# When the experts of a layer pair start, how evenly their work is spread, and how PSUM banks are handed out

## The chip, the cores and the metric

The kernel runs on one core of a Trainium2 chip. A core has five engines with instruction queues of their own: TensorE (PE, matmuls and transposes into PSUM), VectorE (DVE), ScalarE (ACT), GpSimd (POOL) and SyncE (SP, which here only issues DMAs). [...]The metric is the device time of one execution in microseconds (us), lower is better.

## The reference

The input is 16 sequences of 512 tokens with 256 features. Two layers follow each other, each with a residual and a layernorm. All arithmetic is float32.

The first layer is a bidirectional state-space block:

```
xr = x @ in_proj_w.T ; xf, res = split(xr)                # 512 channels each
xf = silu(conv4(xf))   ; y   = ssm(xf, forward weights)
xb = silu(conv4b(xf))  ; y_b = ssm(xb, backward weights, reversed in time)
x = layernorm(x + ((y + y_b) * silu(res)) @ out_proj_w.T)
# ssm: delta = softplus(..); for each of 16 states n:
#   dA = delta * A[n] ; dB_u = delta * u * B[n] ; xs = scaled cumulative sum of dB_u under the decays
#   y += xs * C[n] ; then y += u * D
```

The second layer is a soft mixture of 16 experts with 64 slots each (1,024 slots), with weights of three matrices per expert (256x512, 256x512, 512x256):

```
logits = layernorm(x) @ se.T                              # 512 tokens x 1024 slots
slots  = softmax over tokens (dispatch).T @ layernorm(x)
eout   = (gelu(slots @ Wg + bg) * (slots @ Wu + bu)) @ Wd + bd
x = layernorm(x + softmax over slots (combine) @ eout)
```

## The kernel before

**The scan.** For each sequence `b` of 16 there are four calls of `scan_part` (direction `r`, half of the channels `p`). A part has 8 pairs of states and two chunks of 128 channels, so 16 scan steps; a sequence has 64 and the kernel 1,024. A step does the following. POOL multiplies `du` with the broadcast row `bs` into `db` (L427). ScalarE computes two decays `exp` (L444) and two factors `tanh` (L446). VectorE runs two `tensor_tensor_scan` into the PSUM tiles `h` (L450 forward, L452 backward), each followed by a product with the factor into one half of `hg` (L455). POOL multiplies `hg` with the broadcast row `cs` (L456). PE adds the transposed result into the accumulator `acc` (L371) two steps later. Buffers: `h` 3 PSUM tiles, `th`, `db`, `bs` and `cs` 3 each, `hg` 4. For the states 5 and 13 the term comes from PE instead (`by_diagonal`, L405, from `dg` and `duT`) and lies in a PSUM bank from its matmul to the scan that reads it.

**Side work.** Everything else is written as Python generators, run piece by piece between the scan steps by `beside_scan` (L541). There are three queues, objects of class `Side`: `prep` (projections, convolution taps and steps of the parts to come), `front` (`finish`: output projection, layernorm and `dispatch` of the sequence before) and `back` (`experts` and `combine`). A generator yields the number of PSUM banks that its next piece needs; GAP added to it means not in the step in which something of this queue was taken up; HOLD means that the piece's banks are still to be read, which is done at the next step; WAIT means nothing before the next step. In each step every held or waiting queue is taken up (`take_up`), then `prep` may do a piece, then `front` and `back` each do one if they have at least 1.0 credit. Credit grows each step by the pieces left divided by the scan steps left (`paced_piece`, L524).

**Banks.** Side work and `by_diagonal` share 3 PSUM banks in one rotating pool. `count` numbers all banks handed out, and a piece may run if the number handed out since the oldest hold, with its own need, is at most 3 (L510, L511).

**Layer pairs.** Sequences 2g and 2g+1 share one pass `experts(g)` over all expert weights, in 8 steps of two experts: `pg` (L825, L830), Gelu, `pu` (L779), product, `peo` (L806), store. `combine` of each of the two follows: 4 blocks of tokens with `cl` (L884), Exp, `ctp` (L905) and `cpo` (L962). Slots go through DRAM: `dispatch` writes `s_dram` in four quarters (L738), and `experts` reads them in `load_slots` (`st`, one buffer, L766). `experts(g)` is added at the start of sequence 2g+3, when the dispatch of sequence 2g+1 is complete, to be spread over 128 steps; that of sequences 12 and 13 has only the 64 steps of sequence 15.

**Tail.** Behind the last scan, five more banks and more SBUF come free. `side_by_side` (L1033) then runs `front` and `back` in turns, in three rounds: `finish(15)` beside what `back` has left and the combine weights of sequence 14; the last experts beside the weights of 15; the two combines.

**Order of instructions.** A planner of the framework orders each engine's instructions by program order and its own model of what is ready; an instruction in `late(...)` keeps its place in program order. DMAs of SP are queued in the same way.

## Time and profile before

| What | Value |
|---|---|
| time, median of 3 runs | 5415.38 us (5413.15 to 5421.7) |
| time of the profiled execution | 5411.23 us |
| its span, first to last instruction | 5409.4 us |
| POOL, VectorE, PE, ScalarE busy | 87%, 84%, 80%, 76% |
| mean granted PE clock | 0.889 |
| DMA | 907.7 MB, mean 168 GB/s |

Rows of groups give line, engine, operation, tiles and shapes, the count, busy us, the mean ns of one, and the idle time of the engine ahead of them with what ended it. Rows of stretches give, for a stretch in us from the start of the span, its length, the busy time of each engine with the number of instructions, the granted PE clock, and the share and rate of the DMA engines. Rows of waits give who waited for whom, the us in total, the number of waits and the longest. Rows in order of time give start, duration, engine, line and operation. Queue names with a q (ACTq) are an engine's issue of a DMA.

### The profile page before, as it was taken

How to read it: one execution, taken by the hardware profiler on the slowest of the kernel's cores; microseconds unless marked ns; L12 is line 12 of the kernel's file. 1: busy time of each engine (PE TensorE's matmuls, PEld its weight loads, DVE VectorE, ACT ScalarE, POOL GpSimd, SP SyncE). 2: the span in 40 equal slices, each digit the busy share in tenths (PEclk: the TensorE clock that was granted, in tenths of full speed). 3: DMA queues.
4: the chain of work that ended last, by engine and by line, in shares of the span. 5: the costliest groups of instructions: out<-in, count | busy, mean ns of one | idle time of the engine just before them, and what ended most of it. 6: DMA issues, size and time to landing. Idle time of an engine off the chain costs nothing. (4 is left out here: it accounts for less than half of the span.)

```text
span 5409.4 us, 73721 instructions
## 1 busy us (share of the span) xinstructions
PE 4331.1 (80%) x24144; PEld 3390.0 (63%) x24145; DVE 4559.7 (84%) x6276; ACT 4087.2 (76%) x6515; POOL 4732.1 (87%) x2537
## 2 busy tenths in 40 slices
PE   5656666898888978788888977889787897888889
PEld 3445555676666666677656765667656776667657
DVE  7888988889898899888998888988899889988722
ACT  6677777787888778887877887788788887877641
POOL 6999999999999899998999989998999989988600
PEclk7778778898899988899888989899889998989999
DMA  4334333575446644566446754467444764457436
GB/s 137 131 117 137 125 129 131 189 230 159 156 142 212 225 149 148 158 223 213 131 144 194 232 170 153 132 212 232 149 149 146 225 224 134 145 179 234 126 103 188
DMA packets 595236, 907.73 MB, mean 168 GB/s; under 512 B 78082, under 2 KB 384898, under 8 KB 594852
## 3 DMA queue, kind: packets, MB, share of 16 engines
q1 hardware_dynamic: 521156, 859.87, 49.5%
q10 hardware_dynamic: 73696, 43.14, 2.8%
q8 instruction: 192, 3.15, 0.2%
q14 instruction: 192, 1.57, 0.1%
HBM read 840.86 MB, written 62.01 MB: 167 GB/s over the span
## 5 line engine op out<-in xcount | busy, mean ns | idle before, releaser
L456 POOL TENSOR_TENSOR hg<-hg,cs 128x1024 f32<-128x1024 f32 x1024 | 2420.8, 2368 | 128.1 <-DVE hg L455 110.0
L427 POOL TENSOR_TENSOR db<-du,bs 128x1024 f32<-128x1024 f32 (+1 forms) x1024 | 2144.4, 2098 | 232.3 <-DVE h L450 84.7
L371 PE MATMUL acc<-ident,hg 128*128 128x128 f32 x8192 | 1179.3, 295 | 203.3 <-POOL hg L456 181.6
L455 DVE SCALAR_TENSOR_TENSOR hg<-th,h 128x512 f32<-128x512 f32 x1792 | 1185.8, 678 | 177.2 <-PE acc L371 90.4
L371 PEld LDWEIGHTS acc<-ident,hg 128*128 128x128 f32 x8192 | 1044.9, 154 | 390.8 <-POOL hg L456 240.9
L452 DVE TENSOR_TENSOR_SCAN h<-h,db 128x512 f32<-128x512 f32 x896 | 1072.8, 1218 | 112.2 <-ACT h L444 107.5
L450 DVE TENSOR_TENSOR_SCAN h<-h,db 128x512 f32<-128x512 f32 x896 | 1071.1, 1217 | 48.8 <-ACT h L444 45.7
L446 ACT ACTIVATE th<-rr,Ah_f 128x512 f32<-128x512 f32 x1024 | 725.0, 714 | 186.3 <-DVE hg L455 183.1
L446 ACT ACTIVATE th<-rr,Ah_b 128x512 f32<-128x512 f32 x1024 | 721.5, 712 | 155.2 <-DVE hg L455 147.7
L444 ACT ACTIVATE h<-dt,A_f 128x512 f32<-128x512 f32 x896 | 608.2, 680 | 117.5 <-DVE hg L455 112.6
L444 ACT ACTIVATE h<-dt,A_b 128x512 f32<-128x512 f32 x896 | 608.6, 681 | 108.8 <-DVE hg L455 105.1
L687 PE MATMUL pl<-x2T,seT 128*128 128x512 f32 x512 | 299.1, 715 | 78.7 <-DVE hg L455 37.4
L405 PE MATMUL hd<-dg,duT 128*128 128x128 f32 x2048 | 305.6, 298 | 32.7 <-ACT yt L627 13.5
L830 PEld LDWEIGHTS pg<-st,Wg 128*128 128x128 f32 x2048 | 244.8, 196 | 106.2 <-issue 85.0
L405 PEld LDWEIGHTS hd<-dg,duT 128*128 128x128 f32 x2048 | 283.1, 214 | 38.4 <-ACT yt L627 15.7
L806 PE MATMUL peo<-Wd,ht 128*128 128x256 f32 x1024 | 257.0, 407 | 55.6 <-DVE rr L337 38.6
L779 PE MATMUL pu<-st,Wu 128*128 128x128 f32 x2048 | 254.5, 283 | 50.1 <-DMA Wu<-in_Wu_dram 32.7
L962 PE MATMUL cpo<-ceo,ct 128*128 128x256 f32 x1024 | 254.8, 407 | 46.9 <-DVE rr L337 39.9
L779 PEld LDWEIGHTS pu<-st,Wu 128*128 128x128 f32 x2048 | 244.9, 198 | 61.5 <-DVE h L452 24.2
L830 PE MATMUL pg<-st,Wg 128*128 128x128 f32 x2048 | 269.9, 286 | 4.1 <-DMA Wg<-in_Wg_dram 3.1
L884 PE MATMUL cl<-seT,cx 128*128 128x512 f32 x512 | 244.7, 617 | 32.5 <-DVE res L272 12.3
L806 PEld LDWEIGHTS peo<-Wd,ht 128*128 128x128 f32 x1024 | 205.3, 206 | 97.7 <-DVE rr L337 41.2
(154 smaller groups left out, 6654.8 us busy)
## 6 DMA issues: line engine op xcount, KB each, us to landing
cs<-bc SPq DMA_DIRECT2D x512, 512.0 KB, 3.9
bs<-bc SPq DMA_DIRECT2D x384, 512.0 KB, 5.1
Wg<-in_Wg_dram SPq DMA_DIRECT2D x128, 512.0 KB, 6.0
Wu<-in_Wu_dram SPq DMA_DIRECT2D x128, 512.0 KB, 6.0
Wd<-in_Wd_dram SPq DMA_DIRECT2D x128, 512.0 KB, 5.5
dg<-diag_dram SPq DMA_DIRECT2D x128, 256.0 KB, 4.2
bs<-bc SPq DMA_DIRECT2D x128, 256.0 KB, 3.6
x<-in_x_dram SPq DMA_DIRECT2D x32, 512.0 KB, 6.3
```

The lines of the kernel that those rows point to most:

```text
L371: ins = nc.tensor.matmul(accs[c][:, s], hc[:, j, s], ident, is_transpose=True, start=False, stop=(last and j == 1 and lc == NL - 1),)
L405: ins = nc.tensor.matmul(h[:, s], v[c][3][:, s], dg[:, s], start=True, stop=True)
L427: nc.gpsimd.tensor_tensor(db[:, :k, :], du.unsqueeze(1).to_broadcast([P, k, L]), bs[:, :k, :], ALU.mult)
L444: nc.scalar.activation(hs[j][1], dt, AF.Exp, scale=w["A"][:, c, s])
L446: nc.scalar.activation(ths[j], rr, AF.Tanh, bias=LN_1E12 / 2, scale=w["Ah"][:, c, s])
L450: nc.vector.tensor_tensor_scan(h, dec, add, 0.0, ALU.mult, ALU.add)
L452: nc.vector.tensor_tensor_scan(h[:, ::-1], dec[:, ::-1], add[:, ::-1], 0.0, ALU.mult, ALU.add)
L455: nc.vector.scalar_tensor_tensor(hg[:, j, :], th, 1.0, h, ALU.add, ALU.mult)
L456: nc.gpsimd.tensor_tensor(hg, hg, cs, ALU.mult)
L779: nc.tensor.matmul(pu[:, fc * P : (fc + 1) * P], got["Wu", e][:, k, fc * P : (fc + 1) * P], st[:, k, :, j * SL : (j + 1) * SL], start=(k = ...
L806: nc.tensor.matmul(po[:, j * DM : (j + 1) * DM], ht[:, fc, :], got["Wd", e0 + j][:, fc, :], start=(fc == 0), stop=(fc == NF - 1),)
L830: nc.tensor.matmul(pg[:, fc * P : (fc + 1) * P], got["Wg", e][:, k, fc * P : (fc + 1) * P], st[:, k, :, j * SL : (j + 1) * SL], start=Fals ...
```

## The change

1. **Start of the experts.** `experts(g)` is added at the start of sequence 2g+2 and waits, expert pair by expert pair, until the quarter of the slots that it needs has been written by `dispatch` of sequence 2g+1 (`dispatched`, `ready`). `combine` waits for `expert_done`.
2. **Pace.** `back` gets a fixed 0.4 credit per step; a piece of experts costs 1.1 and one of a combine 0.8. In sequence 15 the pace is again what is left over the steps left.
3. **Banks.** Each bank is a pool tag of its own, and a list `free` says which can be handed out; a piece may run if the list has as many as it needs. In the tail the list gets five more.
4. **Taps.** `turn_back` yields WAIT behind each chunk.
5. **Scans.** A step issues its two scans and then its two products.
6. **Tail.** One round: `back` runs the last experts and the combine of 14, `front` runs `finish(15)`, the weights of 14 and 15 and the combine of 15.

```diff
-        ps = ctx.enter_context(tc.tile_pool(name="m_ps", bufs=3, space=PSUM))
+        ps = ctx.enter_context(tc.tile_pool(name="m_ps", bufs=1, space=PSUM))
...
-        count = [0]
+        free, taken = [0, 1, 2], []
         def bank(name):
-            count[0] += 1
-            if tail and count[0] % 8 >= 3:
-                return tail[0].tile([P, 512], F32, tag="tps", name=name)
-            return ps.tile([P, 512], F32, tag="mps", name=name)
+            i = free.pop(0)
+            taken.append(i)
+            pool = ps if i < 3 else tail[0]
+            return pool.tile([P, 512], F32, tag=f"mps{i}", name=name, bufs=1)
...
                 nc.scalar.copy(xb[:, c, 0 : KW - 1], pb[:, 0 : KW - 1])
+                yield WAIT
             out["u"] = xb
...
                     for j in range(2):
-                        (h, dec, add), th = hs[j], ths[j]
+                        h, dec, add = hs[j]
...
-                        nc.vector.scalar_tensor_tensor(hg[:, j, :], th, 1.0, h, ALU.add, ALU.mult)
+                    for j in range(2):
+                        nc.vector.scalar_tensor_tensor(hg[:, j, :], ths[j], 1.0, hs[j][0], ALU.add, ALU.mult)
...
+                    own = [diags.pop(0)] if k == 1 else []
                     if nxt_n + 1 in DIAG:
                         for x in sides:
                             x.take_up()
+                        if not free:
+                            free.append(own.pop())
                         by_diagonal(nxt_n + 1, chunks[1] if c == chunks[0] else chunks[0])
                     beside_scan()
-                    if k == 1:
-                        diags.pop(0)
+                    free.extend(own)
                     add_up(2)
...
             def go(self):
-                at = count[0]
                 mark = next(self.gens[0][1], None)
-                self.wait = mark == WAIT
-                if mark == HOLD:
-                    self.hold = at if self.hold is None else self.hold
+                self.held += taken
+                taken.clear()
+                self.hold, self.wait = mark == HOLD, mark == WAIT
+                if self.hold:
                     return
-                self.hold, self.gap, self.need = None, False, 0
+                free.extend(self.held)
+                self.held, self.gap, self.need = [], False, 0
...
-                    oldest = min([x.hold for x in sides if x.hold is not None] + diags[:1], default=count[0])
-                    if count[0] - oldest + self.need > BANKS:
+                    if self.need > len(free):
                         break
...
             def paced_piece(self, gaps):
-                self.credit = min(self.credit + sum(x[0] for x in self.gens) / max(self.left, 1), 2.0)
+                rate = self.rate or sum(x[0] for x in self.gens) / max(self.left, 1)
+                self.credit = min(self.credit + rate, 2.0)
                 self.left -= 1
+                weight = self.gens[0][2] if self.gens else 0.0
                 if self.credit >= 1.0 and self.piece(gaps):
-                    self.credit -= 1.0
+                    self.credit -= weight
...
                     nc.scalar.dma_start(s_dram[b, :, :, h * 256 : (h + 1) * 256].rearrange("k p s -> p k s"), sl)
+                    dispatched[b] = h + 1
...
+            def ready(ep):
+                return dispatched.get(b0 + 1, 0) > ep // 2
             prefetch()
-            st = load_slots(lo)
+            st = None
             yield 0
...
             for ep in range(lo, hi):
                 e0 = 2 * ep
+                while not ready(ep):
+                    yield WAIT
+                if st is None:
+                    st = load_slots(ep)
+                    yield WAIT
                 yield 2
...
-                if ep + 1 < hi:
-                    st = load_slots(ep + 1)
+                st = load_slots(ep + 1) if ep + 1 < hi and ready(ep + 1) else None
...
+            expert_done.add(g)
...
         def combine(b, kept=None):
+            while b // 2 not in expert_done:
+                yield WAIT
...
-                cts, sm = kept.pop((b, lc)) if kept else (yield from weights(b, lc, x2, False))
+                while kept is not None and (b, lc) not in kept:
+                    yield WAIT
+                cts, sm = (yield from weights(b, lc, x2, False)) if kept is None else kept.pop((b, lc))
...
-        FINISH, COMBINE, PAIR = 32, 14, 4
+        FINISH, COMBINE, EXPERTS = 32, (13, 0.8), (25, 1.1)
+        back.rate = 0.4
...
-            if b >= 3 and b % 2 == 1:
-                g = (b - 3) // 2
-                back.add(8 * PAIR, experts(g, 0, 8))
-                back.add(COMBINE, combine(2 * g))
-                back.add(COMBINE, combine(2 * g + 1))
+            if b >= 2 and b % 2 == 0:
+                g = b // 2 - 1
+                back.add(EXPERTS[0], experts(g, 0, 8), EXPERTS[1])
+                for i in range(2):
+                    back.add(COMBINE[0], combine(2 * g + i), COMBINE[1])
             hurry = b + 1 == nb
             front.begin(64)
-            back.begin(128 if b % 2 == 1 and b + 1 < nb else 64)
+            if hurry:
+                back.rate = None
+                back.begin(64)
...
-        tail.append(ctx.enter_context(tc.tile_pool(name="t_ps", bufs=5, space=PSUM)))
+        tail.append(ctx.enter_context(tc.tile_pool(name="t_ps", bufs=1, space=PSUM)))
-        BANKS = 8
+        free.extend(range(3, 8))
...
         g, kept = nb // 2 - 1, {}
-        back.add(1, all_weights(2 * g, kept))
-        side_by_side()
-        front.add(1, experts(g, 0, 8))
-        back.add(1, all_weights(2 * g + 1, kept))
-        side_by_side()
-        front.add(1, combine(2 * g, kept))
-        back.add(1, combine(2 * g + 1, kept))
+        back.add(1, experts(g, 0, 8))
+        for b in (2 * g, 2 * g + 1):
+            front.add(1, all_weights(b, kept))
+        back.add(1, combine(2 * g, kept))
+        front.add(1, combine(2 * g + 1, kept))
         side_by_side()
```

## The prediction

> **What bounds the kernel now.** I read the page's first part, then its groups, then the engines' busy time by stretch, the waits inside one stretch, and the order of time at the end.
>
> ```profile
> PE 4331.1 (80%) x24144; PEld 3390.0 (63%) x24145; DVE 4559.7 (84%) x6276; ACT 4087.2 (76%) x6515; POOL 4732.1 (87%) x2537
> ...
> L456 POOL TENSOR_TENSOR hg<-hg,cs 128x1024 f32<-128x1024 f32 x1024 | 2420.8, 2368 | 128.1 <-DVE hg L455 110.0
> L427 POOL TENSOR_TENSOR db<-du,bs 128x1024 f32<-128x1024 f32 (+1 forms) x1024 | 2144.4, 2098 | 232.3 <-DVE h L450 84.7
> ```
>
> Each of the 1,024 scan steps has one L427 and one L456 on POOL: 2098 + 2368 = 4.47 us, so 64 steps of a sequence cannot take less than 286 us. Counting L427 off by 64 gives where each sequence starts, and the stretches below are sequences 2 (no expert or combine work), 11 (experts), 12 (combines), 15 (the last), and three parts of the tail behind the last L456 at 5132.3.
>
> ```profile
> core 0: us, PE busy (x) PEld busy (x) DVE busy (x) ACT busy (x) POOL busy (x), PEclk, DMA share, GB/s
> 635.00:935.20 300.20, 204.42 (x1044) 160.18 (x1044) 262.40 (x322) 226.82 (x361) 292.54 (x153) 0.78 0.39 128
> 3475.90:3805.60 329.70, 283.57 (x1718) 229.52 (x1718) 286.10 (x399) 266.40 (x410) 297.53 (x159) 0.94 0.66 210
> 3805.60:4111.30 305.70, 243.16 (x1304) 185.66 (x1303) 280.35 (x383) 243.76 (x405) 292.72 (x157) 0.89 0.46 143
> 4746.20:5132.30 386.10, 326.55 (x1902) 261.83 (x1901) 300.73 (x440) 279.50 (x442) 304.30 (x161) 0.92 0.57 185
> 5132.30:5178.00 45.70, 41.70 (x194) 30.96 (x192) 13.60 (x37) 14.64 (x32) 3.28 (x8) 0.98 0.38 124
> 5178.00:5248.00 70.00, 56.97 (x197) 33.63 (x196) 15.20 (x40) 31.01 (x67) 1.70 (x4) 0.93 0.14 45
> 5248.00:5370.00 122.00, 121.13 (x735) 95.83 (x735) 30.03 (x91) 26.86 (x47) 0.00 (x0) 1.00 0.73 227
> ```
>
> POOL sets the pace of sequences 2 and 12 (293 busy of 300 and 306). Beside experts it idles 32 us, and in sequence 15, which carries twice the usual side work, 82 us; VectorE is then nearly as full as POOL. In the tail PE is the bound. Who makes POOL wait in sequence 15:
>
> ```profile
> POOL hg L456 <- DVE hg L455: 39.4, 17, 6.3
> POOL db L427 <- DVE h L450: 22.2, 7, 6.6
> ...
> DVE hg L455 <- PE acc L371: 17.1, 12, 4.8
> ```
>
> POOL waits for VectorE, and VectorE, in part, for buffers of hg that PE adds up late because side matmuls stand ahead in its queue. So the side work costs time only through crowding, and two places are crowded: sequence 15 and the tail. The span is 40.7 (before the first step) + 594.3 (sequences 0 and 1) + 300.2 (2) + 3811.0 (3 to 14, 635.2 a pair) + 386.1 (15) + 277.1 (tail) = 5409.4.
>
> **The change, part by part.**
>
> *Start of the experts.* The first quarter of the slots of the pair's second sequence is written long before the whole:
>
> ```profile
> 3981.03 0.37 ACTq L738 DMA_DIRECT2D s_dram<-sl  x1
> 4028.99 0.37 ACTq L738 DMA_DIRECT2D s_dram<-sl  x1
> 4063.90 0.37 ACTq L738 DMA_DIRECT2D s_dram<-sl  x1
> 4129.10 0.36 ACTq L738 DMA_DIRECT2D s_dram<-sl  x1
> ...
> 5177.22 2.16 PE L687 MATMUL pl<-x2T,seT 128*128 128x512 f32 x4
> ...
> 5199.59 0.37 ACTq L738 DMA_DIRECT2D s_dram<-sl  x1
> ...
> 5249.13 2.05 PE L830 MATMUL pg<-st,Wg 128*128 128x128 f32 x16
> ```
>
> In sequence 12 (from 3805.6) the writes are at steps 36, 46 and 54 and at step 3 of the next. Experts need one write for two expert pairs, so they can begin at about step 38 of every even sequence from 2 on, instead of step 8 of the odd ones from 3 on.
>
> *Pace.* 0.4 credit a step at 1.1 a piece is 0.36 expert pieces a step; 24 pieces (3 for each of 8 pairs) and the load take some 66 steps, to step 40 of the odd sequence. Combines cost 0.8, so 0.5 a step; 26 pieces take 52 steps, to step 28 of the next even sequence, 10 steps before the next experts. It fits. What a piece costs comes from sequences: 299.5 without any (mean of 1 and 2), 329.7 with 25 expert pieces, so 1.2 us each; 305.7 with 24 combine pieces, so 0.25 each. Before, a pair costs 635.2 - 599.0 = 36.2; after, the same pieces at nearly the same density, combines a little denser (0.5 a step for 0.4): I take +2 a pair, 12 in all. The last group now puts 11 expert pieces into the even sequence ahead of its own: 11 x 1.2 = +13. Sequences 2 to 14: +25 us.
>
> *DMAs of the moved step.* Each expert pair issues six weight loads, two of st, one of bd and one store, all on SP, in the same number. New is that the first st load of a group is queued directly behind the write it reads (2.6 us to landing by the DMA table, then 4.7 for st); behind it on SP stand the bs and cs loads of coming steps, for which POOL would wait. Three buffers of each cover four steps (18.6 us), so at nothing; without that cover up to 7 us in seven groups, 50 us. The lower end is taken.
>
> *Sequence 15.* Before it holds 25 expert pieces and some 13 combine pieces, and the second combine falls into the tail. Its first three quarters take 279.0 against 225 in sequences 1 and 2: 54 us for 26 pieces, 2.1 each at that crowding. After, 14 expert and 26 combine pieces are left, at 40/64 = 0.62 a step: 14 x 2.1 = 29; the combines between 0.25 (at 0.4 a step) and 2 (the last quarter, 13 pieces, 107.2 - 74.7 = 32, less some 8 for the pipeline that runs dry); nearer the sparse row, 0.7, so 18. 299.5 + 29 + 18 + 8 = 354.5: -32 us.
>
> *Tail.* It loses the second combine of sequence 13: four times 4.32 (cl and ctp) and 3.46 (cpo), less the first cl, 27 us of PE. The last experts no longer wait for a finished first round: slots are first written at 5199.6 but pg starts at 5249.1. Against that, finish(15) has nothing beside it now. On the trace without the foreign matmuls between: first pl 29 us into the tail (45 now), first write at 41, experts from 49. From 41 on PE is full (durations from the chain in order of time: cl of one block 3.45, ctp 0.87, cpo 3.46; of an expert pair pg 2 x 3.03, pu 3.57, peo 3.46): three quarters of dispatch 24, eight weights x 4.32 = 34.6, experts 8 x (6.06 + 3.57 + 3.46) = 104.7, eight cpo x 3.46 = 27.7, sum 191; then 6 from the last cpo to the end and 5 for bubbles: 243.
>
> The row of sequence 2 shows PE's granted clock at 0.78 where PE is busy two thirds of the time, against 0.93 to 1.00 in the tail. The Trainium skill ("TensorE: Matmul & The Clock Gate", Part 1) says more: after one idle window of about 3.4 us the array runs at half rate until it has been busy as long. That speaks against leaving finish(15) alone. It has 17 us of matmuls ahead of the first write: by the row (0.95 / 0.78) 4 us more, by the rule 17. I take 4, since the row is of this kernel, and add 3 for pieces of sequence 15 left over: tail 250, -27 us.
>
> *Banks by name.* The ring counted a bank as taken until the oldest hold ended; now each comes free by itself. Only PE's waits for a bank can go: rows such as peo on rr (38.6 us), cpo on rr (39.9), pyt on xb (59.4) make perhaps 350 us on PE, mostly not passed on. POOL idles 281 us in sequences 2 to 14 (their 4111.2 less its busy time); a quarter of it would be 70. But a fixed name can also wait where a pool could give another bank, at most +20. I take -10, near nothing, as nothing in the trace prices it.
>
> *Backward taps.* By the code a taps piece still comes at every step: what follows WAIT is taken up and run in the same one. Only the Silu behind them moves one step; that chain ends near step 11 of 16, so 0; 4.7 us for each of 16 sequences if it had no room.
>
> *Two scans first.* In the trace the two scans of a step already stand ahead of both L455 in 579 of 1,024 steps; in the other 445 the first L455 comes one scan (1.22 us) later, and h and th are freed later, db one L455 (0.68) earlier. ScalarE waits for just those buffers:
>
> ```profile
> ACT th L446 <- DVE hg L455: 330.8, 295, 5.7
> ...
> ACT h L444 <- DVE hg L455: 217.7, 223, 5.1
> ```
>
> Gain at most the 142 us that POOL's db waits for scans, of which a sixth, 25; loss at most as in the second rival. The steps that have the order already are no slower (4.90 us a step against 5.03), so 0.
>
> Sum: 25 - 32 - 27 - 10 = -44 us: span 5365, profiled time 5367 (it was 5411.2 for 5409.4), and 5370 for the median, which lies 4 above the profiled run.
>
> **Rivals.** *Banks and even spacing give more:* POOL's 281 us fall by a quarter: 5370 + 10 - 70 = 5310. For it: PE's bank waits; against it: they end mostly in idle time of PE that nobody waits for. *ScalarE comes late:* with h and th freed 1.22 us later, scans wait for exp (rows DVE h on ACT h, 107.5 + 45.7 us now). If the 445 steps lose 0.2 us each, +89: 5459. It decides from 44 / 445 = 0.10 us a step on. For it: the 518 waits above; against it: the mean of the 579 steps. *The pace isn't held* with three banks, the remainder piles up in sequence 15 and the combine stays in the tail: nothing gained, 5412.
>
> **How the numbers follow.** A difference under 0.2% (11 us) can't be told from none. My forecast 0.46, more gain 0.21, pace not held 0.11, ScalarE late 0.22. Faster takes the first two, with a little of the third, and less the edge of the first: 0.68; same 0.09; slower 0.23. The forecast's own range is 5335 to 5400 (tail 236 to 265, sequence 15 340 to 375); with the rivals 5305 to 5440.
>
> **What would show it.** Right: pg from about step 38 of even sequences; sequences 3 to 14 near 318 each with less difference between odd and even; sequence 15 near 355; tail near 250 with pg within 55 us of its start and no cl of sequence 13. Wrong: cl of sequence 13 still in the tail; DVE on ACT h well above 150 us; POOL waiting for bs just behind an st load; pd and pl in the tail at a clock near 0.5.

## The result, and the profile after

The changed kernel takes **5482.7 us** (median of four runs, 5481.4 to 5484.5) against 5416.4 for the kernel before on the same chip: a ratio of **1.0122, 95% interval 1.0106 to 1.0138**. It is slower by 66 us, where I had forecast 46 us faster; the time lies 43 us beyond the end of the range with the rivals (5440). The profiled execution took 5481.4 us, its span is 5479.5.

The page of the changed kernel, engines and the two groups of POOL:

```profile
PE 4357.1 (80%) x24136; PEld 3426.3 (63%) x24145; DVE 4568.6 (83%) x6276; ACT 4107.3 (75%) x6534; POOL 4737.7 (86%) x2537
...
L459 POOL TENSOR_TENSOR hg<-hg,cs 128x1024 f32<-128x1024 f32 x1024 | 2419.4, 2366 | 138.8 <-DVE hg L458 93.7
L429 POOL TENSOR_TENSOR db<-du,bs 128x1024 f32<-128x1024 f32 (+1 forms) x1024 | 2142.7, 2096 | 323.3 <-issue 136.8
```

No engine has much more work than before (TensorE is busy 26 us longer, ScalarE 20): POOL's two operations last as long (2366 and 2096 ns), and its busy time is the same within 6 us. Only the idle time ahead of L429 is larger, 323.3 us (232.3 before). The engines' busy time by stretch: sequences 2, 11, 12 and 15, and then the tail in four parts.

```profile
core 0: us, PE busy (x) PEld busy (x) DVE busy (x) ACT busy (x) POOL busy (x), PEclk, DMA share, GB/s
651.20:970.80 319.60, 239.62 (x1349) 193.41 (x1351) 271.21 (x356) 239.04 (x375) 293.44 (x154) 0.84 0.53 164
3579.50:3902.50 323.00, 271.77 (x1541) 213.36 (x1542) 282.33 (x388) 254.21 (x400) 293.70 (x153) 0.90 0.60 180
3902.50:4230.70 328.20, 263.42 (x1476) 206.54 (x1475) 285.27 (x395) 256.58 (x416) 297.27 (x162) 0.90 0.53 167
4879.30:5243.70 364.40, 298.19 (x1680) 239.78 (x1682) 295.76 (x423) 264.88 (x430) 302.75 (x157) 0.91 0.51 159
5243.70:5289.00 45.30, 34.84 (x149) 23.76 (x147) 9.18 (x25) 16.73 (x33) 5.06 (x13) 0.88 0.46 157
5289.00:5340.00 51.00, 50.99 (x306) 41.63 (x306) 11.03 (x33) 19.07 (x27) 0.00 (x0) 1.00 0.72 229
5340.00:5440.00 100.00, 100.00 (x556) 74.96 (x555) 26.77 (x79) 37.81 (x64) 0.00 (x0) 1.00 0.59 181
5440.00:5479.50 39.50, 33.32 (x150) 26.56 (x148) 12.13 (x34) 10.81 (x22) 9.69 (x32) 0.96 0.21 53
```

The steadier pace is there: sequences 11 and 12 now differ by 5 us (24 before). But they differ at the higher level, with 29 and 31 us of idle POOL each (32 and 13 before). Sequence 15 and the tail are shorter, as forecast. Counted off by L429 as in the prediction, the span falls into three stretches:

| us | sequences 0 to 14 | sequence 15 | tail |
|---|---|---|---|
| before | 4705.5 | 386.1 | 277.1 |
| after | 4838.6 | 364.4 | 235.8 |
| difference | **+133.1** | -21.7 | -41.3 |
| forecast | +15 | -32 | -27 |

The whole miss lies in sequences 0 to 14. The waits of the scans and of POOL's first operation over the whole run, first before, then after:

```profile
DVE h L452 <- ACT h L444: 107.5, 94, 6.2
POOL db L427 <- DVE h L450: 84.7, 52, 6.6
POOL db L427 <- issue: 69.2, 33, 3.2
POOL db L427 <- DVE h L452: 57.2, 34, 6.3
DVE h L450 <- ACT h L444: 45.7, 33, 3.4
```

```profile
DVE h L454 <- ACT h L446: 163.5, 105, 6.6
...
POOL db L429 <- issue: 136.8, 61, 5.6
...
POOL db L429 <- DVE h L454: 111.9, 50, 8.1
...
DVE h L452 <- ACT h L446: 110.0, 86, 9.6
...
POOL db L429 <- DVE h L452: 63.0, 53, 4.4
```

VectorE's scans wait for ScalarE's Exp 273.5 us in all (153.2 before), and POOL's L429, which fills the buffers that the scans read, waits behind the scans. This holds for the waits under "issue" too, for which the profile names no releaser: each of the 61 ends 0.13 us behind the end of a scan, and so do all 33 before. In all POOL waits 312 us for scans, and waited 211 before. ScalarE is the obvious suspect, and the question for the experiments is what makes it late. The sum of the waits for Exp is no measure of the loss, though: e3 below waits only 24 us longer than before and loses 71 us in these sequences, and e16 waits 58 us longer and is faster than before.

### The profile page after: what moved, and what is told of

Read it like the earlier page. It is cut to its first block, busy times and chain, and to the rows that moved or that the text cites. A ratio compares the mean times of both kernels' runs of the same rounds, so it can differ in the third digit from the quotient of the medians.

```text
span 5479.5 us, 73609 instructions
## 1 busy us (share of the span) xinstructions
PE 4357.1 (80%) x24136; PEld 3426.3 (63%) x24145; DVE 4568.6 (83%) x6276; ACT 4107.3 (75%) x6534; POOL 4737.7 (86%) x2537
## 4 chain that ended last, share of the span: by engine, by line
DVE 34%; PE 21%; ACT 20%; issue 9%; POOL 3%; DMA 1%; DVEq 0%; SPq 0%; ACTq 0%; POOLq 0%
DVE h L454 9%; DVE hg L458 7%; DVE h L452 7%; ACT h L446 4%; ACT th L448 4%; PE acc L373 3%; PE peo L823 2%; PE pg L852 2%; PE pq L729 2%; ACT L446 2%; PE hd L407 2%; POOL hg L459 2%; DVE hd L454 2%; PE pu L796 1%; PE cl L906 1%
## 5 line engine op out<-in xcount | busy, mean ns | idle before, releaser
L459 POOL TENSOR_TENSOR hg<-hg,cs 128x1024 f32<-128x1024 f32 x1024 | 2419.4, 2366 | 138.8 <-DVE hg L458 93.7
L429 POOL TENSOR_TENSOR db<-du,bs 128x1024 f32<-128x1024 f32 (+1 forms) x1024 | 2142.7, 2096 | 323.3 <-issue 136.8
L448 ACT ACTIVATE th<-rr,Ah_b 128x512 f32<-128x512 f32 x1024 | 725.0, 716 | 184.7 <-DVE hg L458 179.8
L448 ACT ACTIVATE th<-rr,Ah_f 128x512 f32<-128x512 f32 x1024 | 726.1, 716 | 141.6 <-DVE hg L458 135.2
L446 ACT ACTIVATE h<-dt,A_f 128x512 f32<-128x512 f32 x896 | 612.0, 684 | 115.6 <-DVE hg L458 111.2
L446 ACT ACTIVATE h<-dt,A_b 128x512 f32<-128x512 f32 x896 | 609.3, 683 | 95.8 <-DVE hg L458 94.6
L407 PE MATMUL hd<-dg,duT 128*128 128x128 f32 x2048 | 323.6, 308 | 144.0 <-DVE rr L339 52.9
L796 PE MATMUL pu<-st,Wu 128*128 128x128 f32 x2048 | 275.3, 297 | 93.0 <-ACT dis L719 29.9
L796 PEld LDWEIGHTS pu<-st,Wu 128*128 128x128 f32 x2048 | 266.9, 212 | 108.8 <-ACT dis L719 33.0
L729 PE MATMUL pq<-dis,xn 128*128 128x256 f32 x1024 | 261.6, 411 | 65.6 <-DVE xf L199 36.3
L906 PE MATMUL cl<-seT,cx 128*128 128x512 f32 x512 | 258.5, 639 | 38.5 <-ACT duT L357 12.1
L697 PE MATMUL pl<-x2T,seT 128*128 128x512 f32 x512 | 256.1, 623 | 31.6 <-ACT dis L719 7.5
L729 PEld LDWEIGHTS pq<-dis,xn 128*128 128x128 f32 x1024 | 207.7, 208 | 109.1 <-issue 37.6
```

The source lines that it names most:

```text
L407: ins = nc.tensor.matmul(h[:, s], v[c][3][:, s], dg[:, s], start=True, stop=True)
L429: nc.gpsimd.tensor_tensor(db[:, :k, :], du.unsqueeze(1).to_broadcast([P, k, L]), bs[:, :k, :], ALU.mult)
L446: nc.scalar.activation(hs[j][1], dt, AF.Exp, scale=w["A"][:, c, s])
L448: nc.scalar.activation(ths[j], rr, AF.Tanh, bias=LN_1E12 / 2, scale=w["Ah"][:, c, s])
L459: nc.gpsimd.tensor_tensor(hg, hg, cs, ALU.mult)
L729: nc.tensor.matmul(pq[:, k * 256 : (k + 1) * 256], xn[:, lc, k * P : (k + 1) * P], dis[:, lc, :], start=(lc == 0), stop=(lc == NL - 1),)
```

## The experiments

All times are medians; each is compared with runs of the kernel before on the same chip (5412.9 to 5415.9 us). The stretches are those of the profiled run.

| kernel | time, us | ratio (95% interval) | 0 to 14 | 15 | tail |
|---|---|---|---|---|---|
| e1 scans first, alone | 5443.9 | 1.0061 (1.0044 to 1.0077) | 4735 | 382 | 278 |
| e2 change without scans first | 5484.6 | 1.0131 (1.0116 to 1.0146) | 4844 | 364 | 235 |
| e3 free list and named banks, alone | 5465.7 | 1.0096 (1.0081 to 1.0111) | 4777 | 389 | 250 |
| e4 e3 and the new tail | 5461.9 | 1.0095 (1.0074 to 1.0115) | 4775 | 388 | 251 |
| e5 old count, named banks | 5519.9 | 1.0195 (1.0178 to 1.0212) | 4810 | 399 | 264 |
| e6 free list, banks in one pool | 5465.4 | 1.0091 (1.0076 to 1.0106) | 4776 | 384 | 254 |
| e7 e4 with start and pace | 5498.7 | 1.0154 (1.0139 to 1.0169) | 4859 | 366 | 235 |
| e8 old count, new tail | 5385.4 | 0.9948 (0.9931 to 0.9964) | 4702 | 386 | 256 |
| e9 e3, a bank kept for hd | 5494.4 | 1.0153 (1.0136 to 1.0170) | 4797 | 389 | 251 |
| e10 e6, preparation by the old count | 5449.0 | 1.0065 (1.0042 to 1.0088) | 4772 | 382 | 254 |
| e11 e8 with start and pace | 5458.0 | 1.0083 (1.0068 to 1.0098) | 4787 | 386 | 245 |
| e12 change, a bank kept for hd | 5523.0 | 1.0202 (1.0187 to 1.0217) | 4832 | 360 | 284 |
| e13 before, no table loads | 5326.4 | 0.9834 (0.9819 to 0.9848) | 4630 | 372 | 283 |
| e14 e3, no table loads | 5312.6 | 0.9815 (0.9799 to 0.9832) | 4634 | 384 | 248 |
| e15 change, no table loads | 5294.4 | 0.9780 (0.9766 to 0.9795) | 4667 | 350 | 235 |
| e16 before, one number moved | 5390.3 | 0.9949 (0.9934 to 0.9964) | 4672 | 383 | 279 |
| e17 e8 and e16 | **5358.5** | **0.9900** (0.9883 to 0.9916) | 4681 | 387 | 256 |
| e18 change, pieces kept from the loads' steps | 5491.3 | 1.0146 (1.0130 to 1.0161) | 4848 | 364 | 238 |

A profiled run can lie off the median of its kernel, by 15 us in e9 and 13 in e16 (both shorter) and by 8 in e17 (longer); a difference of stretches of that size is not to be relied on.

### The change taken apart: e1 to e8

**e1**, the kernel before with the two scans first:

```diff
-                        nc.vector.scalar_tensor_tensor(hg[:, j, :], th, 1.0, h, ALU.add, ALU.mult)
+                    for j in range(2):
+                        nc.vector.scalar_tensor_tensor(hg[:, j, :], ths[j], 1.0, hs[j][0], ALU.add, ALU.mult)
```

> The kernel before with only the two scans of a step issued ahead of its two products. Theory A (h and th come free one scan later, so ScalarE's exp comes late and VectorE waits for it; 10 and 6 us were lost in sequences 0 and 1, which have no expert or combine work, about 8 a sequence or 130 in all): 5480 to 5545 us, VectorE's wait for exp up from 153 to some 270 us. Theory B (banks by name): 5405 to 5430. Theory C (the loss comes from experts beside dispatch and the even pace): 5405 to 5430.

**e2**, the changed kernel with scan and product in turns, as before:

```diff
-                    for j in range(2):
-                        nc.vector.scalar_tensor_tensor(hg[:, j, :], ths[j], 1.0, hs[j][0], ALU.add, ALU.mult)
+                        nc.vector.scalar_tensor_tensor(hg[:, j, :], th, 1.0, h, ALU.add, ALU.mult)
```

> The changed kernel with scans and products in turns again, all else as changed. Theory A: 5350 to 5420 us, sequences 0 and 1 back at 295 and 299. Theory B and C: 5465 to 5490.

On the kernel before the order of scans costs 30 us, more than two of the theories allowed and less than the third; on top of the rest it makes no difference (5484.6 without, 5482.7 with it). The late Exp of the changed kernel is not its doing: in e2 VectorE waits 149.1 + 90.7 = 239.8 us for it, with the scans in turns.

**e3**, the kernel before with the free list and the named banks alone; **e4**, the same with the new order of the tail (and with an expert pair's slots loaded only when they are ready):

```diff
-            count[0] += 1
-            if tail and count[0] % 8 >= 3:
-                return tail[0].tile([P, 512], F32, tag="tps", name=name)
-            return ps.tile([P, 512], F32, tag="mps", name=name)
+            i = free.pop(0)
+            taken.append(i)
+            pool = ps if i < 3 else tail[0]
+            return pool.tile([P, 512], F32, tag=f"mps{i}", name=name, bufs=1)
...
-                    if count[0] - oldest + self.need > BANKS:
+                    if self.need > len(free):
```

> The kernel before with only the banks by name (with the free list and what goes with it); start of the experts, pace, tail, taps and scans as before. Theory B: 5470 to 5540 us, with sequences 0 and 1 longer by 10 and 6 us. Theory A: 5395 to 5430. Theory C: 5395 to 5430.

> Banks by name and the new tail (last experts beside dispatch, one round), start and pace of the other experts as before. Against e3 it shows the tail alone: 15 to 25 us less than e3, since the second combine of sequence 13 still falls into the tail. Theory A: 5375 to 5410. Theory B: 5450 to 5520. Theory C: 5375 to 5410.

The banks, which I had at -10 us, cost 71 us in sequences 0 to 14 and give 27 back in the tail, where eight banks lie in the list: some 50 us net. That the list did it is read from the edit. The tail was 250 us long with it; the new order of its rounds, from which I expected another 15 to 25 us, adds nothing to that (251 in e4).

**e5**, the old count, but each bank a name of its own in rotation; **e6**, the free list over one pool of three, so that the rule alone is new:

```diff
-            return ps.tile([P, 512], F32, tag="mps", name=name)
+            return ps.tile([P, 512], F32, tag=f"mps{count[0] % 3}", name=name, bufs=1)
```

```diff
-            pool = ps if i < 3 else tail[0]
-            return pool.tile([P, 512], F32, tag=f"mps{i}", name=name, bufs=1)
+            if i < 3:
+                return ps.tile([P, 512], F32, tag="mps", name=name, bufs=3)
+            return tail[0].tile([P, 512], F32, tag=f"mps{i}", name=name, bufs=1)
```

> The kernel before, its counting rule and all else kept, but each of the three banks is a pool tag of its own, handed out in turn. The banks cost 71 us in sequences 0 to 14 of e3; two causes are possible. Theory B1 (the fixed name: the planner can no longer give a matmul whichever bank comes free first): 5445 to 5490 us. Theory B2 (the new rule lets more pieces run, and they crowd): 5400 to 5430 us.

> As e3 (free list, old start, pace, tail, taps and scans), but the three banks are one pool again, so that only the rule of the free list is new. Theory B1: 5380 to 5420 us (sequences as before, the tail 27 us shorter as in e3). Theory B2: 5450 to 5475 us, as e3.

e6 is as slow as e3, so under the free list it is the rule that costs and not the names. Under the old count a fixed name does cost, 104 us, beyond both ranges. As I read it, a bank in a strict rotation must be waited for, where the pool could give another; PE's idle time ahead of one matmul of the scan, hd, goes with that (17 us before, 190 in e5, sequences 1 to 14).

**e7**, everything but scans and taps; **e8**, the kernel before up to the last scan, then the free list of eight banks and the new tail:

```diff
 # e7, on e4
+            if b >= 2 and b % 2 == 0:
+                g = b // 2 - 1
+                back.add(EXPERTS[0], experts(g, 0, 8), EXPERTS[1])
...
 # e8, on e6
+            count[0] += 1
+            if not tail:
+                return ps.tile([P, 512], F32, tag="mps", name=name, bufs=3)
             i = free.pop(0)
```

> All of the change but the scan order and the WAIT behind each backward tap. Against e2 (5484.6) it shows the taps, against e4 (5461.9) the early start and the constant pace. If the WAIT costs (the silu one step later makes what follows late): 5450 to 5465 us. If start and pace cost it: 5475 to 5490 us.

> The kernel before up to the last scan, with the same order on every engine; behind it the free list of eight banks and the new tail in one round. If the tail's gain is its own (e4's tail took 251.1 us for 277.1): 5380 to 5395 us. If it came from what the free list did in sequence 15: 5405 to 5420 us.

Start and pace cost 84 us in sequences 0 to 14 (e7 against e4) and give 39 back behind them; no run separates the two. From e7 to e2 only the WAIT behind the taps is added: 14 us faster, 15 of them in sequences 0 to 14. e8 keeps what the tail gives and pays nothing for it: 30 us faster than before.

### Two theories that fell: e9 to e12

Summed over sequences 1 to 14, the time that PE sits idle ahead of the diagonal matmul hd, waiting for another tile's reader to free its bank, is 17 us before, 83 in e3 and 122 after, and 119 in e5 with 71 more under "issue"; hd is the one matmul on these banks that the scan itself needs. So the leading theory was that hd is handed a bank that has just been let go. Its rival: preparation comes one or two steps earlier under the free list.

**e9** (on e3) and **e12** (on the changed kernel) keep a bank free ahead of hd; **e10** holds preparation back by the old count:

```diff
 # e9, e12
-                    if self.need > len(free):
+                    if self.need > len(free) - keep[0]:
...
+                    keep[0] = int(n + 3 in DIAG)        # e9: and b + 1 < nb
                     beside_scan()
+                    keep[0] = 0
 # e10, on e6
+                    if self is prep and not tail and count[0] - oldest + self.need > 3:
+                        break
```

> The kernel of e3 (free list, a name for every bank, nothing else), with one line more: in the step ahead of a step that issues a diagonal matmul (tile hd), pieces of the side work leave one bank free, in sequences 0 to 14. Theory of the diagonal's bank: under the free list hd is given the bank that a piece has just let go, and waits for its reader in PE's in-order queue with the acc group and the next scan behind it (idle time of PE ahead of hd, sequences 1 to 14: 17 us before, 83 in e3). With a bank kept for it, that falls below 30 us, sequences 0 to 14 go from 4777 back to some 4715, and the time from 5466 to 5405 (5395 to 5420). Rival, the preparation comes too early (its dt operations lie one to two steps earlier under the free list, and add, beside the scan, to ScalarE's and VectorE's queues): the idle time ahead of hd falls, but the time stays within 15 us of 5466.

> The kernel of e6 (the free list's rule over one pool of three banks), but a piece of the preparation may begin only where before's count would have let it, too; expert and combine pieces go by the free list. Rival of early preparation: its dt operations go back to before's steps, and the time from 5465 to 5415 to 5425. Theory of the diagonal's bank: PE's idle time ahead of hd (65 us in e6) falls only as far as the extra rule keeps banks unused, and the time goes down in that share: with 45 to 65 us left there, 5450 to 5466.

> The changed kernel whole, with the one line of e9: a bank kept free for hd in the step ahead. Theory of the diagonal's bank: PE's idle time ahead of hd goes from 122 us to below 40, and the time from 5483 to about 5405 (5385 to 5425), so that start, pace and new tail are then worth about what I forecast. Rival of early preparation: within 20 us of 5483, since pieces only lie a step later here and there.

e9 and e12 are slower than what they started from, and say little of the theory, because the edit did not do what it was for: PE still idles 96 and 87 us ahead of hd, in e9 mostly behind the reads that write xb and res. (e12 also leaves work over, so that its tail is 48 us longer.) e10 answers both questions. First the row of hd in e3, then in e10; the last numbers are the idle time ahead of it in the whole run and what ended most of it.

```profile
L405 PE MATMUL hd<-dg,duT 128*128 128x128 f32 x2048 | 315.6, 304 | 106.5 <-DVE rr L337 49.3 <-ACT cm L913 20.8 <-ACT th L446 19.4
```

```profile
L409 PE MATMUL hd<-dg,duT 128*128 128x128 f32 x2048 | 306.0, 297 | 41.6 <-DVE rr L340 16.8 <-ACT et L718 10.9 <-DVE xf L202 5.5
```

In e10 hd waits hardly longer than before (41.6 against 32.7; in sequences 1 to 14 23 against 17), and the steps of the preparation are nearly before's. Its sequences 0 to 2 take 893.2 us, as before (894.5). Yet sequences 3 to 14, those with expert and combine pieces, take 67 us more (3878.4 against 3811.0), nearly all of what the free list costs. Neither theory can explain that. The theory that side matmuls crowd on PE had gone before: those between two acc groups, counted above 4 us each, fall from some 550 us before to some 400 in e3.

**e11**, e8 with start and pace, without the free list in the scan:

```diff
+        FINISH, COMBINE, EXPERTS = 32, (13, 0.8), (25, 1.1)
+        back.rate = 0.4
```

> The kernel of e8 (before's count of banks up to the last scan, free list and new tail behind it), with the early start of the experts and the constant pace, so that start and pace are seen without the free list. If what start and pace cost (37 us from e4 to e7) is theirs alone - 84 us in sequences 0 to 14, of which 45 come back later - the time is 5385 + 37 = 5422 (5412 to 5432), with ScalarE's table loads up by some 30. If it came out of their meeting with the free list, 5375 to 5395.

Start and pace cost 86 us in sequences 0 to 14 under the old count too (4787 against 4702), so this cost and that of the free list add up. The number of table loads has no part in it (347 against 348 in e8, where I expected 30 more). Here nothing came back in sequence 15, as this kernel is behind with its pieces there: the last group of experts begins at step 56 of sequence 14 instead of step 39. So the time lies 36 us above the 5422 that I expected.

### What ScalarE is late with: e13 to e15

Take every four steps in a row of sequences 3 to 14, counted off by L429, and of ScalarE's work beside the scan in them, table loads counted, what exceeds 9 us: summed and divided by four, that is 35 us before, 70 after and 47 to 92 in the kernels e3, e5 to e7 and e9 to e12. So the side work lies in bunches. ScalarE loads another table for Silu, Softplus and Gelu, where it isn't there already, and the scan's again behind them. The two largest rows of loads before and after, by the line that they precede:

```profile
L444 ACT ACT_TABLE_LOAD x120 | 154.0, 1283 | 2.1
L320 ACT ACT_TABLE_LOAD x64 | 82.1, 1283 | 2.4 <-issue 1.3
```

```profile
L446 ACT ACT_TABLE_LOAD x129 | 165.5, 1283 | 2.3
L322 ACT ACT_TABLE_LOAD x64 | 82.1, 1283 | 2.4 <-issue 1.3
```

All in all 337 loads before and 356 after: 19 x 1.283 = 24 us more on an engine that is busy three quarters of the time, which by itself is no explanation for 133. The number can't be it: e3 has 334, fewer than before, and loses 71 us. The test takes the loads away from three kernels:

```diff
-                    late(nc.scalar.activation(xf[:, c, :], xf[:, c, :], AF.Silu))
+                    late(nc.scalar.activation(xf[:, c, :], xf[:, c, :], AF.Tanh))
...
-                    act = nc.scalar.activation(dt, pz, AF.Softplus)
+                    act = nc.scalar.activation(dt, pz, AF.Exp)
...
-                    args = (ht.rearrange("p f s -> p (f s)"), pg, AF.Gelu)
+                    args = (ht.rearrange("p f s -> p (f s)"), pg, AF.Tanh)
```

> The kernel before, with every Silu and Gelu computed as Tanh and every Softplus as Exp, so that ScalarE never changes its function table beside the scan (337 loads of 1283 ns each before): other values come out, the instructions are the same otherwise. It is the base line for the next two. Theory of the bunches on ScalarE: a step of 4.6 us bears some 3 us of side work on ScalarE; where a Silu, Softplus or Gelu with its two table loads meets another piece's copies, the scan's Exp and Tanh come late. Then 5300 to 5370; if table loads are covered everywhere, above 5400.

> The kernel of e3 (free list and named banks alone) with the same three functions exchanged. Theory of the bunches on ScalarE: what the free list costs in sequences 0 to 14 (71 us in e3 against before) shrinks to below 30 against e13, as most of a bunch is table loads. Rival, the order on TensorE (bank waits and acc groups behind side matmuls): it stays at 55 to 85 us.

> The changed kernel with the same three functions exchanged. Bunches on ScalarE: what the change costs in sequences 0 to 14 (133 us) shrinks to below 60 against e13, and since sequence 15 and the tail still give back some 60, the time is within 20 us of e13's or below it. Rival on TensorE: it stays above 100 us there, and the time some 50 to 70 above e13's.

Each then has one load in the whole run. The stretches of e13 (sequences 0 to 14, sequence 15, tail), the first one of e14, and those of e15:

```profile
40.80:4671.00 4630.20, 3720.42 (x20982) 2916.75 (x20984) 4148.02 (x5615) 3322.94 (x5612) 4409.30 (x2319) 0.89 0.55 171
4671.00:5043.40 372.40, 314.73 (x1877) 256.28 (x1876) 297.82 (x437) 234.01 (x404) 301.81 (x160) 0.94 0.61 191
5043.40:5326.30 282.90, 251.29 (x1248) 187.07 (x1246) 67.53 (x191) 70.90 (x148) 14.72 (x45) 0.95 0.45 139
```

```profile
39.90:4673.70 4633.80, 3661.82 (x20963) 2883.18 (x20976) 4160.80 (x5618) 3324.33 (x5615) 4409.44 (x2319) 0.90 0.55 171
```

```profile
40.40:4707.80 4667.40, 3744.91 (x21261) 2962.07 (x21268) 4170.62 (x5651) 3322.24 (x5626) 4411.56 (x2323) 0.89 0.56 172
4707.80:5058.00 350.20, 295.39 (x1681) 238.73 (x1683) 293.67 (x422) 234.42 (x408) 302.33 (x157) 0.91 0.54 166
5058.00:5293.30 235.30, 218.63 (x1156) 166.65 (x1154) 59.26 (x169) 63.83 (x130) 14.60 (x44) 0.97 0.53 166
```

| sequences 0 to 14, us | with table loads | without | difference |
|---|---|---|---|
| before (e13) | 4705.5 | 4630.2 | 75 |
| free list and named banks, e3 (e14) | 4776.8 | 4633.8 | 143 |
| changed (e15) | 4838.6 | 4667.4 | 171 |
| e3 against before | +71.3 | **+3.6** | |
| changed against before | +133.1 | **+37.2** | |

Without loads the free list costs 4 us and not 71; the changed kernel loses 37 us in sequences 0 to 14 and gains 22 and 48 behind them, and is **32 us faster** than before (5294.4 against 5326.4). So 96 of the 133 us go when the table loads go: 68 of the 71 that the free list costs, and 28 of the 62 that the rest of the change adds in these sequences. Two reservations. Without the loads ScalarE also has some 430 us less to do (337 loads of 1.283 us), and no run takes the same time from it in another way; so it is not shown that it must be loads and not any work of ScalarE at those places. And the planner orders the instructions of these kernels anew, so they differ from the ones with loads by more than the loads. That all three come within 37 us of each other in that stretch, where they lay 133 apart, speaks against chance order alone, but doesn't exclude it.

Where the loads' cost arises can be read from the traces. Take POOL's idle time in sequences 3 to 14, and of it what falls between 1 us ahead of a table load and 9 us behind it (two steps; some 1,500 us of each run lie in such windows): before, 147 of 273 us; in e3, 202 of 328; in e10, 230 of 334; after, 209 of 365. For the free list the whole increase, 55 us in e3, lies beside the loads, and what lies elsewhere is as before (126 and 125). After, 62 us of the increase lie beside them and 30 elsewhere. For start and pace the picture is another one: from e4 to e7 POOL's idle time grows by 62 us, and none of that lies beside the loads (196 and 195); from e8 to e11 it grows by 57, of which 16 lie there. In the windows of Gelu's loads alone, each cut off at the next load away from the scan's table, POOL idles some 45 us before, 120 in e3 and 80 after.

One such place, in sequence 9 of both kernels. ScalarE in the kernel before (start us, us, what it does; in brackets its idle time ahead and what ended it):

```profile
2886.87 1.28 ACT L259 ACT_TABLE_LOAD   x1
2888.16 1.91 ACT L259 ACTIVATE xb<-xb 128x2048 f32<-128x2048 f32 x1
2890.09 1.28 ACT L847 ACT_TABLE_LOAD   x1
2891.39 0.60 ACT L847 ACTIVATE ht<-pg 128x512 f32<-128x512 f32 x1
2891.88 0.59 ACT L850 ACTIVATE ht<-pg 128x512 f32<-128x512 f32 x1
2892.49 1.28 ACT L444 ACT_TABLE_LOAD   x1
2893.78 0.69 ACT L444 ACTIVATE h<-dt,A_f 128x512 f32<-128x512 f32 x1
```

The same work in the changed kernel, on ScalarE, then on VectorE and on POOL:

```profile
2974.39 1.28 ACT L261 ACT_TABLE_LOAD   x1
2975.68 1.91 ACT L261 ACTIVATE xb<-xb 128x2048 f32<-128x2048 f32 x1
2977.61 1.28 ACT L869 ACT_TABLE_LOAD   x1
2981.25 0.60 ACT L869 ACTIVATE ht<-pg 128x512 f32<-128x512 f32 x1 [2.35 <-PE pg L852]
2982.26 0.60 ACT L872 ACTIVATE ht<-pg 128x512 f32<-128x512 f32 x1 [0.42 <-PE pg L852]
2982.76 0.72 ACT L448 ACTIVATE th<-rr,Ah_f 128x512 f32<-128x512 f32 x1
2983.49 1.28 ACT L446 ACT_TABLE_LOAD   x1
2984.79 0.69 ACT L446 ACTIVATE h<-dt,A_f 128x512 f32<-128x512 f32 x1
```

```profile
2976.94 1.24 DVE L452 TENSOR_TENSOR_SCAN h<-h,db 128x512 f32<-128x512 f32 x1
2983.51 0.69 DVE L458 SCALAR_TENSOR_TENSOR hg<-th,h 128x512 f32<-128x512 f32 x1 [5.34 <-ACT th L448]
2985.51 1.23 DVE L452 TENSOR_TENSOR_SCAN h<-h,db 128x512 f32<-128x512 f32 x1 [1.32 <-ACT h L446]
```

```profile
2979.48 2.37 POOL L459 TENSOR_TENSOR hg<-hg,cs 128x1024 f32<-128x1024 f32 x1
2986.88 2.37 POOL L429 TENSOR_TENSOR db<-du,bs 128x1024 f32<-128x1024 f32 x1 [5.03 <-issue]
```

Before, pg is finished when ScalarE gets to it, and the scan's next Exp comes 6.9 us after the first load. After, the queue reaches Gelu too early: with Gelu's table already in, ScalarE waits 2.35 and 0.42 us for pg, Tanh and Exp of the scan stand behind it, and 10.4 us pass. VectorE idles 5.34 us for the Tanh and 1.32 for the Exp; POOL's next L429 starts 0.14 us after that scan's end, having idled 5.03 us, more than a step (one of the 61 waits under "issue"). Here the same stay costs more because of what it waits for. In sum, between a load away from the scan's table and the load back, ScalarE idles ahead of a Gelu 2 us before, 27 in e3 and 17 after (sequences 3 to 14). That is a part, not the whole: it is far less than 62 or 55 us. The rest I take for several small ways in which a stay in another table meets a step without slack, but no trace row adds them up.

### Can the loads be kept apart by rule, and is before's timetable special: e16 to e18

**e16** moves one number of the kernel before:

```diff
             front.begin(64)
+            front.credit = 0.5
```

> The kernel before, with one number changed: the dispatch's credit begins each sequence at 0.5 and not at 0, so that its pieces lie a step or two earlier against the others, and no rule, bank or amount of work changes. If before's timetable is one that happens to lie well, so that any other one costs (the share of the loss that is no property of the free list), it is slower by 30 to 70 us (5445 to 5485). If only the rules of the change cost, it is within 10 us of before.

It gains 24 us, against both expectations (33 in sequences 0 to 14 of a profiled run that was 13 us shorter than the median). Loads fall to 321, and POOL's idle time beside them from 147 to 131 us. So before's timetable is no best one, and that other timetables cost as a matter of course is wrong; but a step or two of one queue moves the time by half a per cent. A difference of that size can come from the timetable alone.

**e17** joins e8 and e16:

```diff
 # on e8
             front.begin(64)
+            front.credit = 0.5
```

> The kernel of e8 (before up to the last scan, free list and new tail behind it) with e16's one number (the dispatch's credit begins at 0.5). The two gains lie in different stretches, 33 us in sequences 0 to 14 and 22 us in the tail, so they should add up: 5416 - 24 - 30 = 5362 (5350 to 5375). If the tail's gain hangs on where the last sequence leaves its pieces, 5370 to 5390.

5358.5 us, ratio 0.9900: the gains add up (24 and 30 us make 54), and this kernel beats both.

**e18**, the changed kernel, in which no other piece begins in a step that issued a Silu, Softplus or Gelu:

```diff
-                if self.credit >= 1.0 and self.piece(gaps):
+                if self.credit >= 1.0 and not skip and self.piece(gaps):
```

> The changed kernel with all its work and its own functions, but in a step in which a Silu, a Softplus or a Gelu was issued (in sequences 0 to 14) no piece of the dispatch, the experts or the combine begins; its credit waits for the next step. Theory of the bunches on ScalarE: the loads stay as many (356, give or take 20), but lie beside less; sequences 0 to 14 give back 30 to 80 of the 133 us, and the time is 5400 to 5455. If only the loads' number or their own time matters and not what lies beside them, it stays within 15 us of 5483; pieces that come later and end up in the tail can add to either, so sequences 0 to 14 decide.

It misses: 5491.3 us, and sequences 0 to 14 take 4848 us. That is where the rival had it, by which only the number of the loads or their own time matters; but the number had been ruled out by e3. The measure that the edit was to mend did fall in part (ScalarE's side work beyond 9 us in four steps, 70 to 59 us), and the time didn't follow; so bunching by the step, as I worded it, is not what decides. The Softplus rows, first in the changed kernel, then in e18, show one place where the cost went:

```profile
L322 ACT ACTIVATE dt<-pz 128x512 f32<-128x512 f32 x64 | 38.3, 598 | 9.2 <-PE pz L313 8.5
```

```profile
L325 ACT ACTIVATE dt<-pz 128x512 f32<-128x512 f32 x64 | 38.2, 598 | 51.4 <-PE pz L316 50.7
```

ScalarE now waits 51 us for pz, in six waits, all directly behind the load of Softplus's table and with the scan's Exp behind them: the same trouble with another function. I take from it that it matters whether the operand is there when the stay in another table begins, which a rule that only spaces pieces doesn't see; no run tests that by itself.

**What stays open.** That 96 us of the loss go with the loads is shown by e13 to e15, within the reservations above. How they divide among waits inside a stay, longer stays (553 us with another table in before, 615 in e3, 584 after, sequences 3 to 14) and steps without slack was only read from traces, not separated by a run. Of the idle time that start and pace bring, little lies beside the loads, and more than half of what the change adds to the free list's cost (34 of 62 us) stays without them; by which path is open.

## Why the prediction was wrong, step by step

Two terms failed. The price of the moved pieces, +25 us, was 84 in sequences 0 to 14, and the banks, -10, cost 71 there before giving 27 back in the tail. The gains that I forecast for sequence 15 and the tail, 59 us, came (63, the tail's in part for another reason), and could not cover that.

- **Start of the experts, and the pace: held.** pg begins at steps 39, 48 and 57 of the even sequences from 6 on; the last combine ends at step 33 or 34 of the next even one, where I had 28. This rival (pace not held) is out, though under the old count (e11) it does happen.
- **Sequences 2 to 14, +25: wrong.** Start and pace cost 84 us (e4 to e7), before the taps take 15 off. I priced a piece by the mean of sequences that the pieces fitted well, 1.2 and 0.25 us each, and carried that to other places. The step that failed is the one that took a piece's price for a property of the piece: the same pieces at other steps added 84 us where I had worked out 25. Part of that hangs on what ScalarE has loaded: without loads the changed kernel lies 34 us above e14, with them 62 above e3. The 34 lie close to my 25, but they hold the taps and the scans too, so that may be luck.
- **DMAs of the moved step, at nothing: stands.** L429 waits 136.8 us under "issue" instead of 69.2, but all these waits end just behind a scan, not behind a late load.
- **Sequence 15, -32: -22.** The mechanism holds; the size was off, as the pieces left for it cost 65 us over the 299.5 of a sequence without them, and not 55.
- **Tail, -27: -41**, and for another reason than I gave. With eight banks in the list the old order of rounds already takes 250 us (e3); with the second combine of sequence 13 gone as well, 236. The course was close: first pl at 27.3 us into the tail (29 forecast), first write of slots at 42.6 (41), pg at 47.4 (49), then 193 us (191). Most of the 18 us that I added for the end, bubbles, clock and left-over pieces was not needed. The clock is told below.
- **Banks by name, -10: +71 in the scan and -27 in the tail.** "Nothing in the trace prices it" was true of the waits on PE that I looked at, and those did hardly change (some 600 us in sequences 1 to 14 before and in e3). What I left out is that a rule on banks decides which step a piece runs in, and so at what point of ScalarE's queue Silu, Softplus and Gelu stand; without the table loads 4 of the 71 us are left. The upper end, +20, was made from waits alone.
- **Taps, 0: -14.** The Silu that moves one step is one of the table changes, and the number of loads falls from 377 (e7) to 358 (e2); by the same oversight I gave it no price.
- **Scans first, 0: +30 alone, none with the rest.** Reading the mean of steps that had the order already was no test of imposing it on the others.
- **ScalarE comes late, the rival at 5459: right row, wrong cause.** Scans wait for Exp 120 us longer, but in e2, with scans in turns, they wait 87 longer as well. The time came out beyond this rival, which itself lay beyond the range that I gave with the rivals (5459 against 5440).

The clock in the tail. I took 4 us for it from the clock of sequence 2, and had 17 by the rule that the Trainium skill's "TensorE: Matmul & The Clock Gate" (Part 1) gives for an idle array. The stretch with the half rate, and the first matmuls in it:

```profile
5264.90:5275.10 10.20, 6.17 (x13) 3.23 (x14) 0.22 (x1) 5.34 (x10) 2.16 (x7) 0.50 0.59 177
```

```profile
5268.92 2.13 PE L676 MATMUL px<-ident,xn 128*128 128x128 f32 x8 [7.30 <-ACT xn L667]
```

PE idles 7.30 us ahead of px. The clock is at 0.50 from 3.3 us into that gap until 6.2 us behind its end, and at 1.00 from there to the end of the 45 us; the mean of 0.88 hides it. So the rule's half rate does set in, after an idle time like the page's 3.4 us, and one of my signs of being wrong was there in part, as 4 us of pl lie in it. But it covers 6.17 us of PE's work and not all 17; as an estimate, half of that, some 3 us, was lost. The 4 was the right size; the 17 had stretched the rule over matmuls behind which the clock was up again.

What I overlooked was in the first profile: 337 loads of 1283 ns on the engine whose Exp the scan waits for. The Trainium skill says it outright ("ScalarE: Activation LUTs", Table sets: the hidden batching unit): group activations by the table set that they need. Spreading the pieces of experts and combines evenly goes the other way. But the rule counts loads, and the 19 more that came are 24 us of ScalarE; what went with the loads grew by 96, and in e3 by 68 with three loads fewer.

## What to carry to other kernels

In a pipeline as full as this one, a side task's price isn't its own length but what it does at the point where it stands in a queue that the loop needs; here that is in part ScalarE's, where a function of another table can hold up the scan until its operand has come and the table is changed back. Before changing when pieces run, list the table loads beside the loop and ask of each whether its operand is ready at the new place. And take what is clear of the loop for itself: the new tail alone, and one number of the pace, made a kernel that beats both, while the change as a whole loses.

## What the hardware showed that I had not expected

- What the table loads cost hangs on where they stand more than on how many there are. Sequences 0 to 14 get shorter without them by 75 us before, by 143 in e3 and by 171 after; the whole runs have 337, 334 and 356 loads.
- Tanh runs on Gelu's table without a load: in the place shown, L448 follows Gelu at 2982.76 directly, and only the Exp of L446 has the load ahead of it. In the changed kernel a Tanh is the next function behind a Gelu 52 times, and never with a load between.
- A load shows as 1283 ns and nothing else beside it: the one at 2890.09 starts 0.02 us behind the operation ahead of it, and Gelu starts 1.30 us after it. The Trainium skill ("ScalarE: Activation LUTs", What ACT_TABLE_LOAD costs) gives 2.66 us for a switch, with a drain of 1.38 us; here a switch takes half of that.
- The granted clock falls to 0.50 inside a single gap of 7.30 us on PE, and is back at 1.00 within 6.2 us of work; a mean over tens of us does not show it.
